# A selective scan whose input products are written where the scan writes, one recurrence ahead, and norms folded into weights

## The chip, the cores and the metric

The program runs on one core of a Trainium2 chip. The core has five engines that work side by side, each with its own queue of instructions: TensorE (PE, matrix products, written to the memory PSUM), VectorE (DVE), ScalarE (ACT), GpSimd (POOL), and SyncE (SP), which here only issues transfers. Operands lie in SBUF, in PSUM or in the chip's main memory (HBM). An instruction waits in its engine's queue until the instructions that it depends on have reported their end; everything behind it in that queue waits too.

The metric is the device time of one execution, in microseconds (us).

## The reference, cut to what matters

The input is four images of 64 channels and 128 x 128 pixels, in float32, and four layers follow one another:

- Layer 0 takes all pixels of all images as one sequence of 65,536 tokens with 64 channels, and applies a selective state-space block (Mamba) with 128 inner channels and 16 states, an output projection, a norm, SiLU, and the residual.
- Layer 1 takes gradients of its input to set a window width, then Fourier-like transforms with small matrix products between them.
- Layer 2 is two 3 x 3 convolutions with batch norm, a channel gate, and the residual.
- Layer 3 is two 3 x 3 convolutions, a Mamba block with 64 states on each image's 16,384 tokens behind a layer norm, and a feed-forward block with a 3 x 3 depthwise convolution behind a second layer norm.

The part that the change touches is the Mamba block and layer 3's norms:

```python
dbl = xc @ x_proj_w.T                   # dt, B and C of each token
delta = softplus(dt @ dt_proj_w.T + dt_proj_b)
def step(h, inp):                       # one token
    d_t, b_t, c_t, u_t = inp
    dA = exp(d_t[..., None] * A)
    h = h * dA + (d_t * u_t)[..., None] * b_t[:, None, :]
    y = einsum('bdn,bn->bd', h, c_t)
    return h, y

def layernorm(x, w, b): return (x - mean) * rsqrt(var + eps) * w + b
t = t + mamba(layernorm(t, ln1_w, ln1_b), ...)
t = t + pvt2ffn(layernorm(t, ln2_w, ln2_b), ...)   # begins with t @ fc1_w.T + fc1_b
```

A Mamba block's input goes through a projection into x and z; x passes a causal convolution of four taps and SiLU and becomes `xc`; the result y is multiplied by SiLU(z).

## The kernel before, in words

**Chunks and iterations.** The class `_Mamba` serves layers 0 and 3. The sequence is cut into chunks of 1024 tokens (TC), 64 in each layer. A recurrence works on one tile of 128 partitions x 1024 tokens: the partitions are 4 states (q) x 32 channels, so that 128 channels are four tiles (j = 0 to 3), and a group of four states (g) is four iterations. Layer 0 has 4 groups, so 16 iterations in a chunk; layer 3 has 16 groups, so 64 iterations.

**An iteration** (in `run`, written out in program order):

1. ScalarE makes `da` = exp(dl x A) (L530), up to four iterations ahead.
2. The input term `bx` = (delta u) x B is made in one of two ways. In an A group ScalarE scales transposed blocks of delta u by B (L373, 32 short passes a group) and TensorE transposes them into PSUM (L470, eight a tile). In a D group TensorE spreads B over the partitions into a PSUM tile `u["B"]` once for the group (L476), and VectorE multiplies it by `du` from SBUF, once an iteration (L561). The product goes to a second PSUM tile, `u["bx"]`, that the group's four iterations use in turn. Layer 0's groups are DADA, layer 3's are DADADAADADADAADA.
3. VectorE runs the scan h = da x h + bx (L567, a `tensor_tensor_scan`), which reads da from SBUF and bx from PSUM, and writes h into one of eight slots of the SBUF tile `ring`.
4. GpSimd multiplies h by C (L570), in the ring's slot and `cb` from SBUF, and writes it back into the slot eight elements lower; once a group it copies the last column of the four slots into `state` (L572).
5. Two and three iterations after a group's end TensorE adds the products over the states into the PSUM tile y (L389), in two halves.

Both PSUM tiles of D groups and those of A groups come from one pool, `bx`, with two buffers. TensorE makes the transposes or the B of iteration i + 1 in iteration i (`produced`).

**Work beside it.** The projections, norms and stores of the chunk before and the chunk ahead are generators (`ahead`, `prepare`, `behind`) that `beside` moves on by pieces between iterations; `yield "wait", k` holds one for k iterations. `pin` fixes each engine's order as written. So nothing is reordered later: what stands behind a late instruction on its engine is late as well.

**Norms of layer 3.** `centred` subtracts the mean with a matrix product, copies the result with ScalarE and squares it; `rstd` makes the reciprocal root; GpSimd multiplies the two (L1273 and L1297); VectorE then applies the norm's scale and term (L1275 into S, the input of the next chunk's projections, and L1299 into o, which the feed-forward reads). S has two columns of the tokens before, zero at an image's begin.

**The gradient stage of layer 1** (L736 to L748) isn't changed; VectorE and GpSimd work there on tiles of some 2048 elements in SBUF.

Of the kernel before, what the change touches and what calls it, by code (L numbers as in the profile page):

```python
# [10 lines left out]
F32 = mybir.dt.float32  # L11
AF = mybir.ActivationFunctionType
ALU = mybir.AluOpType
# [4 lines left out]
P = 128  # L18
B, C, HH, WW = 4, 64, 128, 128
HW = HH * WW  # L20
TC = 1024
# [117 lines left out]
class _Mamba:  # L139
# [19 lines left out]
    def __init__(self, ctx, tc, K, nst, w, kinds, bufs, slots={}):  # L159
        nc = self.nc = tc.nc  # L160
        self.tc = tc
        self.K, self.nst, self.ng, self.kinds, self.bufs = K, nst, nst // NQ, kinds, bufs
        cp = self.cp = ctx.enter_context(tc.tile_pool(name="mc", bufs=1))
        self.wp = ctx.enter_context(tc.tile_pool(name="mw", bufs=2))
        self.dram = ctx.enter_context(tc.tile_pool(name="md", bufs=2, space=DRAM))
        self.bp = ctx.enter_context(tc.tile_pool(name="mb", bufs=1, space=PSUM))
        self.misc = ctx.enter_context(tc.tile_pool(name="mm", bufs=1, space=PSUM))
        self.prev, self.seen = {}, None

        self.slots = slots  # L170

        wx, xpd, dtw = (self.tmp(k)[:n, :DI] for k, n in (("wx", P), ("xpd", 4), ("dtw", 4)))
        for h in range(2):
            nc.sync.dma_start(wx[64 * h : 64 * (h + 1)], w["in_wT"][:, :DI])
        self.taps = []
        for k in range(2):
            cw = cp.tile([P, DI], F32, name=f"cw{k}")
            for h in range(2):
                nc.sync.dma_start(
                    cw[64 * h : 64 * (h + 1)],  # L180
                    w["conv_wT"][2 * k + h : 2 * k + h + 1, :].to_broadcast([64, DI]),
                )
            nc.vector.tensor_mul(cw, wx, cw)
            self.taps.append(cw)
        self.wz = cp.tile([P, DI], F32, name="wz")
        nc.vector.memset(self.wz, 0.0)
        nc.sync.dma_start(self.wz[64:], w["in_wT"][:, DI:])
        self.wbc = cp.tile([P, 2 * nst], F32, name="wbc")
        nc.sync.dma_start(self.wbc, w["xp_bcT"])
        self.wC = cp.tile([P, max(nst, DD)], F32, name="wC")  # L190
        nc.vector.memset(self.wC, 0.0)
        nc.vector.tensor_copy(self.wC[:, :nst], self.wbc[:, nst:])
        self.spread = {}
        for g in (g for g, kind in enumerate(kinds) if kind == "D"):
            s = self.spread[g] = cp.tile([P, P], F32, name=f"spread{g}")
            nc.vector.tensor_copy(
                s.rearrange("p (q e) -> p q e", q=NQ),
                self.wbc[:, NQ * g : NQ * (g + 1)].unsqueeze(2).to_broadcast([P, NQ, DD]),
            )

        nc.sync.dma_start(xpd, w["xp_dt"])
        nc.sync.dma_start(dtw, w["dt_wT"])
        pm = self.pm()
        nc.tensor.matmul(pm[:, :DI], xpd, dtw, start=True, stop=True)
        self.wdt = cp.tile([P, DI], F32, name="wdt")
        nc.vector.tensor_copy(self.wdt, pm[:, :DI])

        cols = {}
        for k in ("conv_b", "dt_b", "D"):
            cols[k] = cp.tile([P, 1], F32, name=f"col_{k}")  # L210
            nc.sync.dma_start(cols[k], w[k])
        self.conv_b, self.dt_b = cols["conv_b"], cols["dt_b"]
        self.dD = cp.tile([P, P], F32, name="dD")
        nc.vector.tensor_scalar(
            self.dD.rearrange("p (j e) -> p j e", j=ND),
            K.eye.rearrange("p (e j) -> p j e", j=ND),
            cols["D"],
            None,
            ALU.mult,
        )  # L220
        self.A = cp.tile([P, ND, self.ng], F32, name="A")
        with nc.allow_non_contiguous_dma(reason="the states on the partitions"):
            for q in range(NQ):
                for j in range(ND):
                    nc.sync.dma_start(
                        self.A[DD * q : DD * (q + 1), j, :],
                        w["A_log"].rearrange("(e j) (g q) -> j q e g", j=ND, q=NQ)[j, q],
                    )
        nc.scalar.activation(self.A, self.A, AF.Exp)
        nc.vector.tensor_scalar_mul(self.A, self.A, -1.0)  # L230
        self.state = cp.tile([P, ND, self.ng], F32, name="state")


        self.ring = cp.tile([P, 2 * ND, GAP + TC], F32, name="ring")

    def pm(self):
        return self.misc.tile([P, TC], F32, name="pm", tag="pm")
# [50 lines left out]
    def inputs(self, c, S, before_silu=None):  # L288

        nc = self.nc  # L290
        xc, sz = c["xc"], c["sz"] = [self.t(k, self.bufs) for k in ("xc", "sz")]
        yield self.slot(c, "z")
        pm = yield from self.halves((self.wz, S[:, 2:]))
        nc.scalar.copy(sz, pm)
        yield self.slot(c, "conv")
        pm = yield from self.halves((self.taps[0], S[:, :TC]), (self.taps[1], S[:, 2:]))

        if before_silu:
            before_silu()
        nc.scalar.activation(xc, pm, AF.Silu, bias=self.conv_b)  # L300
        nc.scalar.activation(sz, sz, AF.Silu)
        nc.scalar.preload_act_table_set(SET6)

    def prepare(self, c):
# [92 lines left out]
    def run(self, chunks, ahead, behind, leads, budget):  # L397
# [109 lines left out]
        for i, (u, j) in enumerate(its):  # L507
# [45 lines left out]
            if full and full[0] <= i:  # L553
                started(behind(full[1], self.gated(full[1])), i)
                full = None
            produced(i + 1)
            if u["kind"] == "D":
                if i == u["at"]:
                    u["bx"] = self.bp.tile([P, TC], F32, name="bx", tag="bx", bufs=2)
                bxs[i] = u["bx"]  # L560
                nc.vector.tensor_mul(bxs[i], u["c"]["du"][j], u["B"])  # L561


            slot = i % (2 * ND)
            hs, hc = self.ring[:, slot, GAP:], self.ring[:, slot, :TC]
            st = self.state[:, j, u["g"] : u["g"] + 1]
            nc.vector.tensor_tensor_scan(  # L567
# [658 lines left out]
def layer3_mamba(ctx, tc, K, w, t3, x3, s3, n3):  # L1226
# [5 lines left out]
    nc.vector.memset(eps, 1e-5)  # L1232
    woT = cp.tile([P, 64], F32, name="woT")
    nc.sync.dma_start(woT, w["out_wT"])
    g1, b1, g2, b2 = (_dup(nc, cp, w[k], f"{k}_") for k in ("ln1_w", "ln1_b", "ln2_w", "ln2_b"))

    def centred(x, out):

        w = x.shape[1]
        pm = yield from m.piece(  # L1240
            *([(lambda pm, a=a: pm[:, a : a + 512], K.cent, x[:, a : a + 512], True, True)] for a in range(0, w, 512))
        )
        nc.scalar.copy(out[0], pm[:, :w])
        nc.scalar.activation(out[1], pm[:, :w], AF.Square)

    tail = cp.tile([P, 2], F32, name="tail")
# [11 lines left out]
    def ahead(c):  # L1258
        if c is chunks[0]:
            load(c)  # L1260
        t0 = c["at"][1]
        S = m.t("S", 1, TC + 2)
        if t0:
            nc.gpsimd.tensor_copy(S[:, :2], tail)
        else:
            nc.gpsimd.memset(S[:, :2], 0.0)
        xs, sq = m.tmp("nxc"), m.tmp("nsq")
        yield from centred(c["X"], (xs, sq))
        if c is not chunks[-1]:
            load(chunks[c["no"] + 1])  # L1270
        yield "wait", 1
        yield from m.rstd(sq, eps)
        nc.gpsimd.tensor_mul(xs, xs, sq)  # L1273
        yield "wait", 2
        nc.vector.tensor_scalar(S[:, 2:], xs, g1, b1, ALU.mult, ALU.add)  # L1275
        if not t0:
            nc.gpsimd.memset(S[:64, 2:3], 0.0)
        nc.gpsimd.tensor_copy(tail, S[:, TC:])
        yield "wait", 1
        yield from m.inputs(c, S)  # L1280

    def behind(c, yg):
        b, t0 = c["at"]
        tr, xr = m.t("tr", 1, 512), m.t("xr", 1, 512)
        for h in range(NH):
            nc.sync.dma_start(tr[64 * h : 64 * (h + 1)], _halves(t3[b], t0)[h])
            nc.sync.dma_start(xr[64 * h : 64 * (h + 1)], _halves(x3[b], t0)[h])
        yield "wait", 2
        pm = yield from m.project(woT, yg, tr)
        nc.scalar.copy(tr, pm[:, :512])  # L1290
        nc.gpsimd.tensor_add(xr, xr, tr)
        yield "wait", 1
        xs, o = m.t("ncr", 1, 512), m.t("o", 1, 512)
        yield from centred(tr, (xs, o))
        yield "wait", 1
        yield from m.rstd(o, eps)
        nc.gpsimd.tensor_mul(o, xs, o)  # L1297
        yield "wait", 2
        nc.vector.tensor_scalar(o, o, g2, b2, ALU.mult, ALU.add)  # L1299
        for h in range(NH):  # L1300
            nc.sync.dma_start(_halves(s3[b], t0)[h], xr[64 * h : 64 * (h + 1)])
            nc.sync.dma_start(_halves(n3[b], t0)[h], o[64 * h : 64 * (h + 1)])
# [6 lines left out]
def layer3_ffn(ctx, tc, K, w, n3, s3, out):  # L1309
# [26 lines left out]
        nc.sync.dma_start(dwb[half[h]], w["dw_b"][:P, :].rearrange("(i q) o -> q (i o)", i=2))  # L1336
    b1 = cp.tile([P, 2], F32, name="ff_fc1_b")
    nc.sync.dma_start(b1, w["fc1_b"].rearrange("(t q) o -> q (t o)", t=2))
    dwb1 = cp.tile([P, 1], F32, name="dwb1")
    nc.sync.dma_start(dwb1, w["dw_b"][P:, :])  # L1340
    nc.sync.dma_start(dww, w["dw_w"].rearrange("(t q) k -> q t k", t=2))
# [212 lines left out]
```

## Time and profile before

| | us |
|---|---|
| median of three runs (20296.65 to 20302.4) | 20297.79 |
| the profiled execution | 20302.69 |
| its span, first to last instruction | 20300.9 |
| VectorE busy | 16466.5 (81%) |
| ScalarE busy | 15261.9 (75%) |
| TensorE busy | 14900.1 (73%) |
| GpSimd busy | 13717.9 (68%) |
| scans, L567 (5120 in the program) | 11153.5 + 610.5 |
| D products, L561 (2304) | 2829.4 |
| GpSimd's products, L570 (5120) | 12134.3 |
| norms' scale and term, L1275 and L1299 (64 each) | 50.7 and 33.4 |

The page shows the span in 40 slices of 507.5 us. Layer 0 fills the first seven, layers 1 and 2 slices 8 to 13, layer 3's Mamba block slices 14 to 37, and the feed-forward block the rest. A digit is an engine's busy share of a slice in tenths. In a row of instructions, the name is line, engine, operation, and tiles (out<-in), with partitions x elements; behind the bar stand busy time, the mean of one in ns, and the engine's idle time just before them with what ended most of it. A timeline's row begins with its start and its length in us.

### The profile page before, as it was taken

The numbers are of one execution on the slowest core, as the hardware profiler recorded it, in microseconds if no ns is written. First come the engines' busy times: TensorE is split into PE (matmuls) and PEld (weight loads), VectorE is DVE, ScalarE is ACT, GpSimd is POOL, SyncE is SP. The second block draws the span as 40 slices with busy tenths as digits, with TensorE's granted clock in tenths as the row PEclk, the third lists the DMA queues.
The fourth block names the chain that finished last, engine by engine and source line by source line (L and its number), as shares of the span: only waits on it lengthen the run. The fifth ranks groups of instructions, "written<-read, shape, count | busy, mean of one in ns | idle before, by whom it ended". The sixth has DMA issues, their size and how long they took to land. (4 is left out here: it accounts for less than half of the span.)

```text
span 20300.9 us, 233291 instructions
## 1 busy us (share of the span) xinstructions
PE 14900.1 (73%) x77130; PEld 7474.5 (37%) x77130; DVE 16466.5 (81%) x9208; ACT 15261.9 (75%) x31389; POOL 13717.9 (68%) x7390
## 2 busy tenths in 40 slices
PE   7777777348798677777777777777777777777677
PEld 3333333147635333333333333333333333333222
DVE  6888888842112799999999999999999999999765
ACT  7888888501122898888898988988989988889522
POOL 6777777710000788888888888888888888888400
PEclk8989998659899888888888888888888888888899
DMA  5555555400121323323323233233232332332211
GB/s 132 143 146 149 145 144 148 96 28 34 39 67 49 80 77 81 86 74 84 82 77 84 77 81 86 74 84 82 77 84 77 82 86 73 84 81 78 57 44 40
DMA packets 687937, 1723.07 MB, mean 85 GB/s; under 512 B 196784, under 2 KB 249344, under 8 KB 681344
## 3 DMA queue, kind: packets, MB, share of 16 engines
q1 hardware_dynamic: 686720, 1708.15, 32.0%
q8 instruction: 605, 9.91, 0.2%
q14 instruction: 612, 5.01, 0.1%
HBM read 1434.79 MB, written 272.63 MB: 84 GB/s over the span
## 5 line engine op out<-in xcount | busy, mean ns | idle before, releaser
L570 POOL TENSOR_TENSOR ring<-ring,cb 128x1024 f32<-128x1024 f32 x5120 | 12134.3, 2388 | 2673.5 <-DVE ring L567 1927.0
L567 DVE TENSOR_TENSOR_SCAN ring<-da,state,bx 128x1024 f32<-128x1024 f32 x4848 | 11153.5, 2336 | 802.6 <-PE bx L470 451.1
L373 ACT ACTIVATE bxT<-duT,BT 128x128 f32<-128x128 f32 x22528 | 7058.0, 387 | 0.0
L530 ACT ACTIVATE da<-dl,A 128x1024 f32<-128x1024 f32 x5120 | 5868.0, 1146 | 1418.2 <-DVE ring L567 1267.6
L470 PE MATMUL bx<-cst,bxT 128*128 128x128 f32 x22528 | 4106.6, 339 | 3093.9 <-DVE bx L561 2526.1
L470 PEld LDWEIGHTS bx<-cst,bxT 128*128 128x128 f32 x22528 | 3473.0, 215 | 4814.7 <-DVE ring L567 1574.0
L389 PE MATMUL y<-ring,cst 128*32 128x512 f32 x20480 | 3560.2, 632 | 311.6 <-POOL ring L570 294.0
L561 DVE TENSOR_TENSOR bx<-du,bx 128x1024 f32<-128x1024 f32 x2304 | 2829.4, 1228 | 225.1 <-DMA du<-d 67.4
L389 PEld LDWEIGHTS y<-ring,cst 128*32 128x32 f32 x20480 | 545.9, 110 | 1863.0 <-POOL ring L570 961.4
L476 PE MATMUL bx<-xc,spread 128*128 128x512 f32 x2304 | 1144.8, 619 | 46.0 <-DVE ring L567 45.0
L1093 PE MATMUL cv<-img,cw 64*64 64x512 f32 x9216 | 1008.0, 594 | 75.2 <-DMA img<-d_x 46.3
L1024 POOL TENSOR_TENSOR xs<-xs,cl 128x1024 f32<-128x1024 f32 x32 | 75.0, 2342 | 1149.6 <-DVE cl L1023 1149.6
L1367 POOL MEMSET h<- 128x18 f32 x64 | 8.3, 132 | 1138.7 <-DVE g L1410 794.2
L1254 POOL MEMSET X<- 64x1 f32 x4 | 0.4, 93 | 1123.0 <-DMA cw<-in_l_conv_wT 1123.0
L1093 PEld LDWEIGHTS cv<-img,cw 64*64 64x64 f32 x9216 | 489.5, 134 | 591.6 <-issue 482.4
L476 PEld LDWEIGHTS bx<-xc,spread 128*128 128x128 f32 x2304 | 390.9, 189 | 830.1 <-DVE ring L567 508.9
L1423 PE MATMUL pd<-h,diag 64*64 64x512 f32 x4608 | 670.5, 629 | 0.7 <-issue 0.7
L567 DVE TENSOR_TENSOR_SCAN ring<-da,bx 128x1024 f32<-128x1024 f32 x272 | 610.5, 2277 | 58.0 <-PE bx L470 42.2
L1007 ACT COPY O<-p 128x1024 f32<-128x1024 f32 x32 | 32.4, 1012 | 803.4 <-PE p L1000 803.4
L1410 DVE SCALAR_TENSOR_TENSOR g<-h,dww,g 128x2048 f32<-128x2048 f32 x256 | 602.0, 2351 | 9.2
L1381 ACT ACTIVATE h<-ph,ff_fc_b 128x384 f32<-128x384 f32 (+1 forms) x384 | 200.1, 574 | 543.9 <-PE ph L1376 543.9
L245 PE MATMUL pm<-xc,wC 128*32 128x512 f32 (+1 forms) x512 | 192.0, 839 | 556.6 <-ACT pos L311 554.2
(309 smaller groups left out, 13655.2 us busy)
## 6 DMA issues: line engine op xcount, KB each, us to landing
cb<-c SPq DMA_DIRECT2D x5120, 128.0 KB, 2.9
dl<-d SPq DMA_DIRECT2D x2048, 128.0 KB, 4.1
du<-d SPq DMA_DIRECT2D x2048, 128.0 KB, 4.4
d<-pos SPq DMA_DIRECT2D x128, 512.0 KB, 2.6
d<-dus SPq DMA_DIRECT2D x128, 512.0 KB, 3.0
X<-d_t SPq DMA_DIRECT2D x124, 256.0 KB, 4.0
S<-in_x SPq DMA_DIRECT2D x120, 256.5 KB, 4.9
res<-in_x SPq DMA_DIRECT2D x128, 128.0 KB, 3.0
```

The costliest lines, as they stand in the source:

```text
L373: nc.scalar.activation(t[:, k, q].rearrange("p e j -> p (e j)"), c["duT"][:, k, :], AF.Copy, scale=c["BT"][:, k, n : n + 1])
L389: nc.tensor.matmul(c["y"][DD * j : DD * (j + 1), _COLS[h]], K.sel, hc[:, _COLS[h]], start=False, stop=u["g"] == self.ng - 1,)
L470: nc.tensor.transpose(bx[:, P * k : P * (k + 1)], v["bxT"][:, k, :, :, j].rearrange("p q e -> p (q e)"), self.K.eye)
L476: nc.tensor.matmul(bx[:, k], self.spread[v["g"]], v["c"]["xc"][:, k], start=True, stop=True)
L530: nc.scalar.activation(das[nexp], v["c"]["dl"][k], AF.Exp, scale=self.A[:, k, v["g"] : v["g"] + 1])
L561: nc.vector.tensor_mul(bxs[i], u["c"]["du"][j], u["B"])
L567: nc.vector.tensor_tensor_scan(hs, das.pop(i), bxs.pop(i), 0.0 if u["c"].get("reset") else st, ALU.mult, ALU.add)
L570: nc.gpsimd.tensor_mul(hc, hs, u["cb"])
L1093: nc.tensor.matmul(p[i][half[h]], W[half[i], k, :], src[half[i], at : at + 4, dx : dx + WW], start=k == 0, stop=k == 8,)
L1381: nc.scalar.activation(himg[:, h * HR + a : h * HR + e, 1 : WW + 1], ph[:, h, a - q : e - q, :], AF.Identity, bias=b1[:, t : t + 1],)
L1410: nc.vector.scalar_tensor_tensor(g1, tap, wk, g1, ALU.mult, ALU.add)
L1423: nc.tensor.matmul(pd[i][half[h]], diag[half[i], k, :], h0[half[i], r : r + 4, dx : dx + WW], start=k == 0, stop=k == 8,)
```

## The change

Three things change.

*D products.* A D group takes no second PSUM tile. The product of an iteration goes into the ring's slot that the scan will write, and the scan reads it from there, in place. The products are issued one recurrence ahead: at j = 0 those of j = 0 and 1, at j = 1 and 2 the next, at j = 3 none.

```diff
             produced(i + 1)
+            slot = i % (2 * ND)
             if u["kind"] == "D":
-                if i == u["at"]:
-                    u["bx"] = self.bp.tile([P, TC], F32, name="bx", tag="bx", bufs=2)
-                bxs[i] = u["bx"]
-                nc.vector.tensor_mul(bxs[i], u["c"]["du"][j], u["B"])
-            slot = i % (2 * ND)
+                for k in range(j + (j > 0), min(j + 2, ND)):
+                    bxs[i - j + k] = self.ring[:, (i - j + k) % (2 * ND), GAP:]
+                    nc.vector.tensor_mul(bxs[i - j + k], u["c"]["du"][k], u["B"])
             hs, hc = self.ring[:, slot, GAP:], self.ring[:, slot, :TC]
```

*The first norm.* Its scale goes into ScalarE's copy of the centred values. Its term is left out of S and added where the projections' results are read: `shift` multiplies the term by the convolution's taps and by z's weights once, and the two SiLU take the result as bias. So that the columns before an image's begin still mean zero, they now hold minus the term.

```diff
+    def shift(self, b):
+        for k, ws in (("conv_b", self.taps), ("z_b", [self.wz])):
+            pm, col = self.pm(), self.cp.tile([P, 1], F32, name=f"{k}_shift")
+            for i, wt in enumerate(ws):
+                self.nc.tensor.matmul(pm[:, :1], wt, b, start=i == 0, stop=i == len(ws) - 1)
+            self.nc.vector.tensor_scalar(col, pm[:, :1], getattr(self, k), None, ALU.add)
+            setattr(self, k, col)
...
-        nc.scalar.activation(sz, sz, AF.Silu)
+        nc.scalar.activation(sz, sz, AF.Silu, bias=self.z_b)
...
-        nc.scalar.copy(out[0], pm[:, :w])
+        nc.scalar.activation(out[0], pm[:, :w], AF.Copy, scale=scale)
...
-            nc.gpsimd.memset(S[:, :2], 0.0)
+            nc.gpsimd.tensor_copy(S[:, :2], pad.to_broadcast([P, 2]))
...
-        nc.gpsimd.tensor_mul(xs, xs, sq)
+        nc.gpsimd.tensor_mul(S[:, 2:], xs, sq)
+        if not t0:
+            nc.gpsimd.tensor_copy(S[:64, 2:3], pad[:64])
+        nc.gpsimd.tensor_copy(tail, S[:, TC:])
         yield "wait", 2
-        nc.vector.tensor_scalar(S[:, 2:], xs, g1, b1, ALU.mult, ALU.add)
-        if not t0:
-            nc.gpsimd.memset(S[:64, 2:3], 0.0)
-        nc.gpsimd.tensor_copy(tail, S[:, TC:])
-        yield "wait", 1
```

*The second norm.* Its scale goes into the feed-forward's first weights and its term, through those weights, into their bias, once before the first strip; `behind` stores GpSimd's product.

```diff
-        yield "wait", 2
-        nc.vector.tensor_scalar(o, o, g2, b2, ALU.mult, ALU.add)
+        yield "wait", 3
...
+    g, n = (_dup(nc, cp, w[k], f"ff_{k}") for k in ("ln2_w", "ln2_b"))
+    ph = hp.tile([P, 2, 4, WW], F32, name="ph", tag="ph")
+    for t in range(2):
+        nc.tensor.matmul(ph[:, t, 0, :1], f1[half[0], t, :], n[half[0]], start=True, stop=True)
+    nc.vector.tensor_add(b1, b1, ph[:, :, 0, 0])
+    nc.vector.tensor_scalar(f1, f1, g, None, ALU.mult)
```

More of the change, by code (lines that the diff above doesn't have):

```diff
@@ L211, in __init__ @@
             nc.sync.dma_start(cols[k], w[k])
-        self.conv_b, self.dt_b = cols["conv_b"], cols["dt_b"]
+        self.conv_b, self.dt_b, self.z_b = cols["conv_b"], cols["dt_b"], 0.0
         self.dD = cp.tile([P, P], F32, name="dD")
@@ L1234, in layer3_mamba, with centred @@
     nc.sync.dma_start(woT, w["out_wT"])
-    g1, b1, g2, b2 = (_dup(nc, cp, w[k], f"{k}_") for k in ("ln1_w", "ln1_b", "ln2_w", "ln2_b"))
-    def centred(x, out):
+    g1, b1 = (_dup(nc, cp, w[k], f"{k}_") for k in ("ln1_w", "ln1_b"))
+    m.shift(b1)
+    pad = cp.tile([P, 1], F32, name="pad")
+    nc.vector.tensor_scalar_mul(pad, b1, -1.0)
+    def centred(x, out, scale=1.0):
         w = x.shape[1]
@@ L1265, in ahead @@
         else:
-            nc.gpsimd.memset(S[:, :2], 0.0)
+            nc.gpsimd.tensor_copy(S[:, :2], pad.to_broadcast([P, 2]))
         xs, sq = m.tmp("nxc"), m.tmp("nsq")
-        yield from centred(c["X"], (xs, sq))
+        yield from centred(c["X"], (xs, sq), g1)
         if c is not chunks[-1]:
```

## The prediction, on record before the changed kernel ran

> **What bounds the kernel now.** I read the slices first. VectorE is at nines in slices 15 to 37, which is layer 3's recurrence; layer 0's (slices 1 to 7) has it at eights.
>
> ```profile
> DVE  6888888842112799999999999999999999999765
> POOL 6777777710000788888888888888888888888400
> ```
>
> Then the same as a table over inner stretches of both stages (PE, PEld, DVE, ACT, POOL busy):
>
> ```profile
> 978.00:3709.00 2731.00, 2153.95 (x10062) 996.75 (x10058) 2283.78 (x1222) 2397.91 (x4607) 2138.09 (x1129) 0.90 0.57 146
> 6900.00:18680.00 11780.00, 8509.86 (x40434) 4218.77 (x40432) 11189.35 (x5848) 10572.87 (x22787) 9925.19 (x5305) 0.85 0.31 81
> ```
>
> In layer 3 VectorE is busy 95%, ScalarE 90%, GpSimd 84%. The scans recorded from 7000 to 18500 us (3614 + 192) are 59.5 chunks of 64, so a chunk takes 11500 / 59.5 = 193.3 us; GpSimd works 0.8425 x 193.3 = 162.9 us of it. Layer 0's stretch holds 376 products, 8 in a chunk: 47 chunks, 58.1 us each, with 45.5 us of GpSimd.
>
> Third, the groups: the scan, the D product before it, GpSimd's product behind it.
>
> ```profile
> L570 POOL TENSOR_TENSOR ring<-ring,cb 128x1024 f32<-128x1024 f32 x5120 | 12134.3, 2388 | 2673.5 <-DVE ring L567 1927.0
> L567 DVE TENSOR_TENSOR_SCAN ring<-da,state,bx 128x1024 f32<-128x1024 f32 x4848 | 11153.5, 2336 | 802.6 <-PE bx L470 451.1
> L561 DVE TENSOR_TENSOR bx<-du,bx 128x1024 f32<-128x1024 f32 x2304 | 2829.4, 1228 | 225.1 <-DMA du<-d 67.4
> ```
>
> Fourth, VectorE's timeline in layer 3: two D recurrences and a run of eight A scans (start, us).
>
> ```profile
> 10023.89 1.23 DVE L561 TENSOR_TENSOR bx<-du,bx 128x1024 f32<-128x1024 f32 x1
> 10025.22 2.35 DVE L567 TENSOR_TENSOR_SCAN ring<-da,state,bx 128x1024 f32<-128x1024 f32 x1
> 10027.60 1.23 DVE L561 TENSOR_TENSOR bx<-du,bx 128x1024 f32<-128x1024 f32 x1
> 10028.93 18.01 DVE L567 TENSOR_TENSOR_SCAN ring<-da,state,bx 128x1024 f32<-128x1024 f32 x8
> ```
>
> A D recurrence costs 10027.60 - 10023.89 = 3.71 us: the scan starts 1.33 after its product and the next product 2.38 after the scan, each waiting for the other's result. Scans with no such wait follow at (18.01 - 2.35) / 7 = 2.24 us. GpSimd's own timeline beside that A run:
>
> ```profile
> 10033.90 9.41 POOL L570 TENSOR_TENSOR ring<-ring,cb 128x1024 f32<-128x1024 f32 x4
> 10043.23 0.22 POOL L572 COPY state<-ring 128x4 f32<-128x4 f32 x1
> 10043.38 9.38 POOL L570 TENSOR_TENSOR ring<-ring,cb 128x1024 f32<-128x1024 f32 x4
> ```
>
> Its pitch is 2.34 us: in A groups it falls behind the scans and catches up only in D groups, where 3.71 leaves it idle 1.36 each time.
>
> The view that decides is the timeline of layer 1's gradient stage, the one place where VectorE has operations with two SBUF inputs while GpSimd works.
>
> ```profile
> 3837.81 4.63 POOL L736 TENSOR_TENSOR v<-X 128x2112 f32<-128x2112 f32 x1 [7.49 <-DMA X<-d_x]
> ...
> 3849.17 2.28 DVE L743 TENSOR_TENSOR gy<-d 128x2048 f32<-128x2048 f32 x1
> ...
> 3891.25 6.74 POOL L739 TENSOR_TENSOR d<-X 128x2112 f32<-128x2112 f32 x1
> 3893.43 6.71 DVE L743 TENSOR_TENSOR gy<-d 128x2048 f32<-128x2048 f32 x1
> 3897.95 6.54 POOL L747 TENSOR_TENSOR gx<-gx,gy 128x2048 f32<-128x2048 f32 x1
> 3900.06 6.58 DVE L741 TENSOR_TENSOR gx<-v 128x2048 f32<-128x2048 f32 x1
> ```
>
> Alone, L743 takes 2.28 us and a GpSimd operation of this size 4.63. Together each takes 6.5 to 6.7, one starting 2.2 after the other, in strict turns: the pair's period is 3900.06 - 3893.43 = 6.63, the sum of both. They exclude each other; what VectorE adds is 6.63 - 4.59 (the pitch of GpSimd's L736 to L739 alone, 3837.81 to 3842.40) = 2.04 us for 2048 elements.
>
> **What the Trainium skill says.** "SBUF — State Buffer", section "Who interferes with whom": a DVE instruction with two SBUF inputs contends with a GpSimd instruction that reads SBUF, since its second input comes through the read interface that both share; section "SBUF: two separate sides" calls it an exclusive lock for the whole instruction. The gradient stage agrees (6.63 above). The first section also says that a DVE instruction with at most one SBUF input, outside the 2-port modes, does not contend: the trace agrees, since scans (da in SBUF, bx in PSUM) and GpSimd's products run side by side at 2.35 and 2.37 us. It names no scan; none with two long SBUF inputs runs beside GpSimd here, so its case is inferred.
>
> **The change part by part.**
>
> *The order.* Product, product, scan, product, scan, product, scan, scan. No scan follows its own product at once, and no product waits for a scan that reads its destination. The product then costs what yg (L593: PSUM and SBUF in, SBUF out) does between starts, 1.14 us (980.46 to 981.60), the scan 2.24: 3.38 for 3.71, a gain of 0.33 x 2304 = 760 us of VectorE if nothing else held it. The product still reads one operand from PSUM, so it doesn't contend. Product j+1 now stands ahead of scan j, and so does its wait for du; du's waits are 67 us in all, and its loads are issued several iterations ahead: 0, at worst these 67 again. Its ring slot was last used eight iterations back; 0 while GpSimd is under three behind.
>
> *The place.* The D scan's second input moves from PSUM to the ring, SBUF. It now has two SBUF inputs, and each of GpSimd's products reads two. By the gradient stage they exclude each other: 2304 scans, each holding the port for about 2.1 us (2.04 for 2048 elements; the scan's pitch of 2.24 us for 1024 says two cycles for each, so as long). The unknown is this hold: 0 if scans don't take the port, 2.35 if it lasts to the scan's end. I take 2.1.
>
> What is late next is GpSimd, which everything waits for: products feed PE's sums (L389), and behind the sums in PE's order stand the next group's transposes or B. So its work and the holds cannot overlap, and its backlog from A groups has nowhere to go. Layer 3, a chunk: 162.9 + 28 x 2.1 = 221.7, plus some 2.5 in which GpSimd waits for neither's turn (first products of D groups, which start 2.52 after their scan, as 9998.79 to 10001.31 now, though the port is free at 2.1: 0.4 x 7) = 224.2, against 193.3: +30.9 x 64 = +1978 us. Layer 0: 45.5 + 8 x 2.1 = 62.3, plus 3 that stay of GpSimd's present longest gap (5.8 to 6.8 us where yg waits for PE, less a hold and what PE gains while D runs slower), 65.3 against 58.1: +7.2 x 64 = +461 us. The 760 of VectorE are not lost but hidden: VectorE no longer sets the pace.
>
> *PSUM's bx.* D groups need one buffer where they took two, so the next A group's transposes can run before the D group ends. L567's waits for PE (451 us) shrink; behind GpSimd this is worth 0, without the contention at most some 250.
>
> *The norms.* L1275 (64 x 0.71 us between starts) and L1299 (64 x 0.44) go: 74 us of VectorE, 0 on the path if GpSimd sets it. The scale in ScalarE's copy: the same pass, 1.01 us. GpSimd's product count stays; its few small copies change by under 10 us in all. S is ready about an iteration earlier: 0.
>
> *Setup.* Matmuls of one column, [P,1] additions, a scaling of 256 elements; the four ln2 loads move from before layer 3 into the feed-forward's start, ahead of dww on SP's queue: 4 x 0.6 issue, +3 us.
>
> Sum: 1978 + 461 + 3 = +2442 on the profiled execution's 20302.7 (span 20300.9): 22745; the median stands 5 below it: 22740.
>
> **The rivals.**
>
> *No contention (0.10): faster.* The scan might take its inputs otherwise than a tensor_tensor. Then layer 3's chunk loses 28 x 0.33 = 9.2, 1.15 of norms and some of 2.9 waits for PE (177.7 / 61): to about 182, above ScalarE's 173.5: -11.3 x 64 = -723. Layer 0, whose waits for PE stay, some -2 x 64 = -130. 19450. It decides if the hold is under about 1.0 us: (193.3 - 162.9 - 2.5) / 28 = 1.0 in layer 3, and layer 0 has 58.1 - 45.5 - 3 = 9.6 / 8 = 1.2, so below this GpSimd stays under the old pace.
>
> *Port shared element by element (0.05): about the same.* The scan needs an element every second cycle; GpSimd might take the others and lose half: 28 x 1.05 = 29.4, so 192 a chunk beside 193.3. 20300, within 250.
>
> *GpSimd's backlog is absorbed (0.13): slower, by less.* Only the D recurrence's own length counts: 2.1 + 2.34 = 4.44 for 3.71, +0.73 x 2304 = 1680, less some 100 of waits and norms: 21880. Against it: GpSimd has no slack in A groups (2.34 for 2.24) and 162.9 of 193.3 in all.
>
> **How the numbers follow.** The full ledger has 0.72; its own range is 22250 to 23350 (a hold of 2.04 to 2.35 gives -138 to +576; the gaps of 2.5 and 3 us, from none to double, 352 either way). With the absorbed case the range is 21700 to 23400. Chances: slower 0.72 + 0.13 + 0.01 = 0.86, within 0.2% (about what a measurement of this kernel tells from no change) 0.03, faster 0.11.
>
> **What would show it.** Right: the groups split into scans with "bx" at 2.34 us and 2304 scans with "ring" as second input well above it, 3.5 us or more in the mean, waiting included; GpSimd's L570 mean rising from 2.39 to about 3.2 and GpSimd busy over 95% in layer 3, with D recurrences 4.4 us apart; layer 3's chunk near 224, layer 0's near 65. Products near 1.2 us show the order's gain was real. Wrong: ring scans at 2.35 and GpSimd's products at 2.39; then 19450. A chunk near 218 with idle GpSimd means absorption.

## The result and the profile after

The changed kernel takes 22418.3 us (median of four, 22415.2 to 22419.3) where the kernel before takes 20297.5: 1.1044 of it, 95% interval 1.1025 to 1.1063. That is slower by 2121 us, 322 less than forecast and inside the range. The profiled execution's span is 22416.7 us.

The slices of the changed kernel: VectorE is at nines as before, and GpSimd is at eights in layer 3 and up to nines in layer 0.

```profile
DVE  7889888822116999999999999999999999999866
POOL 7998889700005888888888888888888888888600
```

Two inner stretches (PE, PEld, DVE, ACT, POOL busy), layer 0 and layer 3:

```profile
978.00:3709.00 2731.00, 2121.66 (x9379) 1012.00 (x9382) 2433.82 (x1135) 2233.23 (x4276) 2459.75 (x1049) 0.86 0.53 136
7500.00:20000.00 12500.00, 8391.31 (x37338) 3963.37 (x37337) 11778.88 (x5288) 9799.54 (x21038) 10970.88 (x4900) 0.81 0.27 70
```

In layer 3 GpSimd's share rises from 84 to 88%, and ScalarE's falls from 90 to 78%: it waits for the others now. VectorE's stays near 95%, but what fills it is shown by the groups, by form:

```profile
L576 DVE TENSOR_TENSOR_SCAN ring<-da,state,ring 128x1024 f32<-128x1024 f32 x2184 | 7463.2, 3432 | 0.0
L576 DVE TENSOR_TENSOR_SCAN ring<-da,state,bx 128x1024 f32<-128x1024 f32 x2664 | 6078.0, 2327 | 948.1 <-PE bx L479 898.2 <-ACT da L539 31.6 <-ACT bxT L382 11.1
L571 DVE TENSOR_TENSOR ring<-du,bx 128x1024 f32<-128x1024 f32 x2304 | 2723.7, 1203 | 283.5 <-PE bx L485 183.9 <-DMA du<-d 92.1 <-issue 3.3
```

The scans of A groups, with bx in PSUM, take 2.33 us as ever. Those of D groups, with their input in the ring, are recorded at 3.43. The product is 0.025 us shorter. GpSimd's groups:

```profile
L579 POOL TENSOR_TENSOR ring<-ring,cb 128x1024 f32<-128x1024 f32 x5120 | 13148.2, 2591 | 2203.3 <-DVE ring L576 1837.0 <-PE bx L479 204.5 <-DMA cb<-c 66.6
L581 POOL COPY state<-ring 128x4 f32<-128x4 f32 x1280 | 1354.0, 1058 | 0.0
```

In the mean its products are up from 2.39 to 2.59 us, and the copy of four elements from 0.20 to 1.06. Where this comes from, one D group shows; first VectorE's timeline, then GpSimd's over the same time.

```profile
12037.48 2.33 DVE L571 TENSOR_TENSOR ring<-du,bx 128x1024 f32<-128x1024 f32 x2
12039.73 3.83 DVE L576 TENSOR_TENSOR_SCAN ring<-da,state,ring 128x1024 f32<-128x1024 f32 x1
12043.48 1.19 DVE L571 TENSOR_TENSOR ring<-du,bx 128x1024 f32<-128x1024 f32 x1
12044.60 3.68 DVE L576 TENSOR_TENSOR_SCAN ring<-da,state,ring 128x1024 f32<-128x1024 f32 x1
12048.20 1.19 DVE L571 TENSOR_TENSOR ring<-du,bx 128x1024 f32<-128x1024 f32 x1
12049.31 5.88 DVE L576 TENSOR_TENSOR_SCAN ring<-da,state,ring 128x1024 f32<-128x1024 f32 x2
```

```profile
12041.34 2.20 POOL L581 COPY state<-ring 128x4 f32<-128x4 f32 x1
12043.78 2.35 POOL L579 TENSOR_TENSOR ring<-ring,cb 128x1024 f32<-128x1024 f32 x1 [0.24 <-PE bx L479]
12048.45 2.35 POOL L579 TENSOR_TENSOR ring<-ring,cb 128x1024 f32<-128x1024 f32 x1 [2.32 <-DVE ring L576]
```

GpSimd's products of the A group end at 12041.3. Only then does the first scan run, to 12043.56, and GpSimd's tiny copy behind it is recorded at 2.20 us. The product from 12043.78 to 12046.13 comes next; the second scan, recorded from 12044.60, ends at 12048.28, so it runs 2.15 us after the product's end. The engines take turns, 4.71 us from scan to scan (12044.60 to 12049.31), where a D recurrence cost 3.71. The fourth scan follows the third at once: no product stands between them, so VectorE is back before GpSimd has seen the third scan's end, and GpSimd's two products from 12053.12 on take 6.56 us.

It is the same all through layer 3. GpSimd's means mix two cases, as the rows over the whole run show (behind the count, min/median/max in ns):

```profile
L581 POOL COPY state<-ring x1280: 180/202/2309, 92.8 to 21174.3; 128x4 f32<-128x4 f32 x183
L579 POOL TENSOR_TENSOR ring<-ring,cb x5120: 2334/2375/4442, 79.6 to 21172.0; 128x1024 f32<-128x1024 f32 x197
```

The medians are nearly those of before (195 and 2372). But 550 copies took over 2 us and 567 products over 3: they met a scan. Where GpSimd meets it between two of its operations, it pauses. From 7500 to 20000 us it pauses 624 times for more than 0.6 us, and in each of these pauses a D scan ends, 2.11 to 2.16 us after GpSimd's last operation.

By layer, from the first scan's start to the last one's (layer 0 has 1024 scans, layer 3 has 4096; last column the whole span):

| us | layer 0 | a chunk | layer 3 | a chunk | span |
|---|---|---|---|---|---|
| before | 3727.5 | 58.2 | 12368.7 | 193.3 | 20300.9 |
| changed | 4003.9 | 62.6 | 14210.3 | 222.0 | 22416.7 |

### The profile page after: what moved, and what is told of

The parts are those of the page before. It is cut to its first block, busy times and chain, and to the rows that moved or that the text cites. A ratio compares the mean times of both kernels' runs of the same rounds, so it can differ in the third digit from the quotient of the medians.

```text
span 22416.7 us, 233249 instructions
## 1 busy us (share of the span) xinstructions
PE 15674.7 (70%) x77140; PEld 7666.3 (34%) x77140; DVE 18564.3 (83%) x9085; ACT 15312.0 (68%) x31389; POOL 16443.8 (73%) x7390
## 5 line engine op out<-in xcount | busy, mean ns | idle before, releaser
L579 POOL TENSOR_TENSOR ring<-ring,cb 128x1024 f32<-128x1024 f32 x5120 | 13148.2, 2591 | 2203.3 <-DVE ring L576 1837.0
L576 DVE TENSOR_TENSOR_SCAN ring<-da,state,ring 128x1024 f32<-128x1024 f32 x2184 | 7463.2, 3432 | 0.0
L576 DVE TENSOR_TENSOR_SCAN ring<-da,state,bx 128x1024 f32<-128x1024 f32 x2664 | 6078.0, 2327 | 948.1 <-PE bx L479 898.2
L479 PE MATMUL bx<-cst,bxT 128*128 128x128 f32 x22528 | 4211.5, 339 | 3547.9 <-DVE ring L576 2070.1
L398 PE MATMUL y<-ring,cst 128*32 128x512 f32 x20480 | 4162.2, 672 | 681.8 <-POOL ring L579 678.3
L571 DVE TENSOR_TENSOR ring<-du,bx 128x1024 f32<-128x1024 f32 x2304 | 2723.7, 1203 | 283.5 <-PE bx L485 183.9
L398 PEld LDWEIGHTS y<-ring,cst 128*32 128x32 f32 x20480 | 651.8, 114 | 2618.2 <-POOL ring L579 1636.7
L581 POOL COPY state<-ring 128x4 f32<-128x4 f32 x1280 | 1354.0, 1058 | 0.0
```

What stands on the lines that cost most here:

```text
L398: nc.tensor.matmul(c["y"][DD * j : DD * (j + 1), _COLS[h]], K.sel, hc[:, _COLS[h]], start=False, stop=u["g"] == self.ng - 1,)
L479: nc.tensor.transpose(bx[:, P * k : P * (k + 1)], v["bxT"][:, k, :, :, j].rearrange("p q e -> p (q e)"), self.K.eye)
L571: nc.vector.tensor_mul(bxs[i - j + k], u["c"]["du"][k], u["B"])
L576: nc.vector.tensor_tensor_scan(hs, das.pop(i), bxs.pop(i), 0.0 if u["c"].get("reset") else st, ALU.mult, ALU.add)
L579: nc.gpsimd.tensor_mul(hc, hs, u["cb"])
L581: nc.gpsimd.tensor_copy(self.state[:, :, u["g"]], self.ring[:, slot - j : slot + 1, GAP + TC - 1])
```

## The experiments

Two questions were open. The first is whether the port is the cause. The *port theory* says that a D scan with two SBUF inputs and a GpSimd operation that reads SBUF exclude each other; its rivals are that a scan from the ring, or in place, is slow by itself, or that running ahead moved a wait. The second is what the order and the norms' edits are worth where the port is out of the way. Every time below stands beside 20299 to 20310 for the kernel before on the same chip.

### The parts apart

The norms' edits alone, on the kernel before. Its D products are kept; the lines show what differs from the changed kernel:

```diff
-                for k in range(j + (j > 0), min(j + 2, ND)):
-                    bxs[i - j + k] = self.ring[:, (i - j + k) % (2 * ND), GAP:]
-                    nc.vector.tensor_mul(bxs[i - j + k], u["c"]["du"][k], u["B"])
+                if i == u["at"]:
+                    u["bx"] = self.bp.tile([P, TC], F32, name="bx", tag="bx", bufs=2)
+                bxs[i] = u["bx"]
+                nc.vector.tensor_mul(bxs[i], u["c"]["du"][j], u["B"])
```

> The norms' edits alone, D products as before. If VectorE sets layer 3's pace before the change, its 64 x 0.71 and 64 x 0.44 us leave the path: 74 us, 20224. If they were covered, 20297. A value above 20300 would mean that the edits cost something elsewhere (three iterations of waiting, transfers at the feed-forward's start).

Measured 20311.0 us, ratio 1.0008 (1.0000 to 1.0016): nothing came off. VectorE's work did fall, but its waits took its place. The same stretch of layer 3, before and with the norms' edits (third column VectorE):

```profile
7500.00:18000.00 10500.00, 7588.90 (x36056) 3762.86 (x36053) 9973.01 (x5214) 9426.60 (x20315) 8848.80 (x4732) 0.85 0.31 81
```

```profile
7500.00:18000.00 10500.00, 7588.68 (x36050) 3786.80 (x36048) 9909.71 (x5102) 9432.14 (x20306) 8813.95 (x4730) 0.85 0.30 81
```

TensorE's, ScalarE's and GpSimd's columns are the same to 0.7% or better, VectorE's is 63 us lower: the chunks pass at the old rate, so VectorE's work alone wasn't the pace.

The D products' edit alone, norms as before:

```diff
-                if i == u["at"]:
-                    u["bx"] = self.bp.tile([P, TC], F32, name="bx", tag="bx", bufs=2)
-                bxs[i] = u["bx"]
-                nc.vector.tensor_mul(bxs[i], u["c"]["du"][j], u["B"])
+                for k in range(j + (j > 0), min(j + 2, ND)):
+                    bxs[i - j + k] = self.ring[:, (i - j + k) % (2 * ND), GAP:]
+                    nc.vector.tensor_mul(bxs[i - j + k], u["c"]["du"][k], u["B"])
```

> The D products' edit alone, norms as before. Port theory (D scans and GpSimd's reads exclude each other, and GpSimd's work plus the holds fill the chunk): VectorE's 74 us of norms come back but are mostly hidden, 22420 to 22490. If the norms' edits did part of the slowing, clearly below 22400.

Measured 22481.3 us, ratio 1.1077 (1.1060 to 1.1094): the whole loss is in this part, and the norms' edits, worth nothing alone, are worth 63 us here (22481.3 - 22418.3; layer 3's stretch is 14290.8 us with the norms' operations and 14210.3 without). The second norm's operation gives a likely reason, in the groups of this kernel:

```profile
L1299 DVE TENSOR_SCALAR o<-o,ln_w__37345,ln_b__37348 128x512 f32<-128x512 f32 x64 | 158.8, 2482 | 9.7 <-POOL o L1297 9.7
```

It took 0.52 us before; here it waits for GpSimd too: 63 of the 64 end 0.28 us after the end of a GpSimd product. It has one SBUF tensor; the Trainium skill, "SBUF — State Buffer", section "Who interferes with whom", lists `tensor_scalar` among the operations that can take the shared port in a 2-port mode, and 2.48 us beside 0.52 agrees. How this becomes 63 us isn't shown: what GpSimd loses beside the two norms' operations (its products there are recorded at 2.85 and 2.52 us for 2.38) is some 40.

The place without the order, on the changed kernel:

```diff
-                for k in range(j + (j > 0), min(j + 2, ND)):
-                    bxs[i - j + k] = self.ring[:, (i - j + k) % (2 * ND), GAP:]
-                    nc.vector.tensor_mul(bxs[i - j + k], u["c"]["du"][k], u["B"])
+                bxs[i] = self.ring[:, slot, GAP:]
+                nc.vector.tensor_mul(bxs[i], u["c"]["du"][j], u["B"])
```

> The changed kernel, but each D product is issued just ahead of its own scan, still into the ring. Port theory: the place decides, so no faster than 22418. The pause between two scans of a D group then always lets GpSimd in, also ahead of the fourth, which follows the third at once in the changed kernel: 1.33 + 3 x 4.7 + 2.25 = 17.7 for a group's 16.8, 576 groups: up to +520, 22400 to 22950. If running ahead is what costs (a wait that moved), below 21500.

Measured 22371.8 us, ratio 1.1023 (1.1008 to 1.1038), 28 below the lowest value that was expected and 47 below the changed kernel: the added turns cost nothing. The place alone makes the loss; running ahead under contention is worth nothing (layer 3 28 us better with it, layer 0 47 us worse, where single executions with the same layer 0 differ by up to 25 us: 4003.9 in the changed kernel, 3979.0 in the run before this one). That the fourth scan slips in at once saves no time; a likely reason is that GpSimd has that work still to do.

### The port taken away

GpSimd's product is replaced by a filling of the same place, which reads nothing; in the changed kernel and, as a control, in the kernel before.

```diff
-            nc.gpsimd.tensor_mul(hc, hs, u["cb"])
+            nc.gpsimd.memset(hc, 0.0)
```

> The changed kernel, but GpSimd fills its half of the ring's slot with zeros where it multiplied by C (the product by C is left out): it writes the same place at the same point of the order and reads nothing. Port theory: D scans no longer wait, 2.3 us each for 3.4, D recurrences 3.38 us apart, 19300 to 19700. If a scan is slow because its input lies in SBUF or because it works in place, it stays slow: 22000 or more.

> The kernel before with the same filling in place of the product by C (left out here too): the control. GpSimd isn't what sets the pace before the change, so 20100 to 20300. Port theory: the changed kernel's counterpart is faster than this one by 500 to 850 us, the sign of the change turned round; otherwise slower by about 2100.

Measured 20128.7 us (0.9913, 0.9899 to 0.9928) and 20195.2 us (0.9947, 0.9932 to 0.9962). The changed kernel becomes 2290 us faster. That is not the contention's price alone, since a filling takes GpSimd 0.96 us where a product takes 2.34; the control's 108 us say what the lighter work is worth only where GpSimd doesn't set the pace. What tells is the scans' own time. The D scans of layer 3, min/median/max in ns, in the changed kernel and then without GpSimd's reads:

```profile
L576 DVE TENSOR_TENSOR_SCAN ring<-da,state,ring x1240: 2317/3642/4529, 7496.4 to 17983.4; 128x1024 f32<-128x1024 f32 x178
```

```profile
L576 DVE TENSOR_TENSOR_SCAN ring<-da,state,ring x1456: 2318/2343/4324, 7516.9 to 17992.8; 128x1024 f32<-128x1024 f32 x182
```

So a scan from the ring and in place is as fast as one from PSUM, 2.34 us, as long as GpSimd doesn't read. The few at 4.3, 169 of 2304 in both layers, all stand beside GpSimd operations that still do (L347 and L355 most of all), and these work on other tiles: it isn't the shared ring that makes the two engines meet. A GpSimd operation that only writes doesn't get in the way: 502 of the D scans ran beside a whole filling, in 2.32 us. A filling as long as the product wasn't tried. D recurrences are 3.38 us apart there (12018.58 to 12021.95 to 12025.33), as worked out. The sign turns, as the port theory says: 66 us faster than the control. The size does not: 500 to 850 were expected. Some contention is left: the 169 scans cost VectorE some 270 us, 164 of them in layer 3. VectorE also waits longer: in layer 3 its work, these 164 included, is 206 us shorter than the control's (11740 to 11534), its pauses are 144 longer (526 to 670). In the whole run it waits 889.5 us before A scans, 767.2 of them for TensorE's transposes.

TensorE's granted clock also fell with the change, from 0.85 to 0.81 in layer 3's stretches. It isn't the cause: without GpSimd's reads it is 0.83, lower than before too, and that run is the fastest.

### GpSimd's slack

Two more passes a chunk in layer 3, 300 us in all, on a tile that nothing reads any more:

```diff
         nc.gpsimd.tensor_add(xr, xr, tr)
+        for _ in range(2):
+            nc.gpsimd.tensor_mul(yg, yg, yg)
```

> The changed kernel with two more passes of GpSimd over 128 x 1024 elements a chunk in layer 3, on a tile that nothing reads any more: 64 x 2 x 2.34 = 300 us of GpSimd work. If its work and the holds fill each chunk, all of it shows: +300, 22720. If VectorE's own alternation with it sets the pace and GpSimd has slack, +0 to 100.

> The kernel before with the same two passes: the control. GpSimd has 30 us of 193 to spare in a chunk, so 0 to +60.

Measured 22615.0 us for the changed kernel, 197 more, and 20326.5 us for the kernel before, 24 more (ratio 1.0011, 1.0005 to 1.0018). In layer 3's stretch it is +216 and +9. GpSimd sets most of the pace after the change and none before; about a quarter of added work still finds room.

### D groups without a second SBUF input

On the norms' edits: B is spread anew for every iteration, and the product replaces it in its PSUM tile.

```diff
-            if v["kind"] == "A" or i == v["at"]:
-                bx = bxs[i] = self.bp.tile([P, TC], F32, name="bx", tag="bx", bufs=2)
+            bx = bxs[i] = self.bp.tile([P, TC], F32, name="bx", tag="bx", bufs=2)
...
-            elif i == v["at"]:
-                v["B"] = bx
+            else:
                 for k in _COLS:
...
-                nc.vector.tensor_mul(bxs[i], u["c"]["du"][j], u["B"])
+                nc.vector.tensor_mul(bxs[i], u["c"]["du"][j], bxs[i])
```

> The norms' edits with another form of D group: TensorE spreads B anew for each iteration, and the product replaces B in its own PSUM tile, so that a product no longer waits for the scan before it, and no scan has a second SBUF input. A D recurrence then costs 1.33 + 2.26 = 3.59 for 3.71: 0.12 x 2304 = 276 us, and 74 of norms: 19950 if TensorE's extra 1728 x 1.24 us stay hidden; 20200 or more if the new B comes late (it can start only when the scan two before has ended).

Measured 20349.2 us, ratio 1.0026 (1.0016 to 1.0035): no gain, as expected if B comes late. Layer 3's stretch falls by 74 us against before (12294.5), layer 0's rises by 114 (3841.4): there products wait 225 us for B, before 8, and the product by SiLU(z) (yg) waits 287, before 232.

### What sets the pace before

These were meant to lighten ScalarE in layer 3 by leaving out SiLU and with it two table loads a chunk; in the kernel before, with the norms' edits, and in the changed kernel without GpSimd's reads (the product by C left out there as well).

```diff
-        nc.scalar.activation(xc, pm, AF.Silu, bias=self.conv_b)
-        nc.scalar.activation(sz, sz, AF.Silu)
-        nc.scalar.preload_act_table_set(SET6)
+        f = AF.Silu if self.slots else AF.Identity
+        nc.scalar.activation(xc, pm, f, bias=self.conv_b)
+        nc.scalar.activation(sz, sz, f)
+        if self.slots:
+            nc.scalar.preload_act_table_set(SET6)
```

> The kernel before with a lighter burst of ScalarE in layer 3: the two SiLU of a chunk become plain copies with bias (SiLU is left out), so that both table loads of 1.28 us go: 64 x 2.56 = 164 us of ScalarE. VectorE's own work is unchanged. If VectorE's work alone set the pace, 0. If ScalarE's bursts hold A groups back, up to -164: 20140.

> The same lightening (SiLU left out in layer 3) with the norms' edits. They brought nothing in front of the full burst. If ScalarE's burst swallowed their 74 us, this run is up to 74 below the one without the norms' edits; if something else paces both, equal.

> The changed kernel with GpSimd's filling in place of the product by C and the lightened burst of ScalarE in layer 3 (product by C and SiLU left out). If ScalarE is what took the order's gain of up to 760 us once the contention was gone, more than its own 164 us come off 20129: 19800 to 19960. If TensorE or the pieces' order took it, 0 to -164.

Measured 20667.7 us (1.0176, 1.0160 to 1.0191), 20532.7 us (1.0107, 1.0090 to 1.0124) and 20367.2 us (1.0028, 1.0019 to 1.0038): all slower. The profile tells that the edit did the reverse of what it was for. Without the preload of a table set that holds both functions, a logarithm and an exponential that follow one another in layer 3 each load their own; the table loads of the lightened kernel before:

```profile
L132 ACT ACT_TABLE_LOAD x132 | 169.4, 1283 | 50.1 <-DMA c_b__31453<-in_l_c_b 41.0 <-issue 3.9 <-DMA bn_v__31471<-in_l_bn_v 2.9
L133 ACT ACT_TABLE_LOAD x132 | 169.4, 1283 | 2.3
L532 ACT ACT_TABLE_LOAD x65 | 83.4, 1283 | 4.8 <-DMA dl<-d 3.7
L315 ACT ACT_TABLE_LOAD x64 | 82.1, 1283 | 1.2
```

The kernel before has five loads each on L132 and L133. In all there are 254 more loads, 326 us of ScalarE. Read that way it is an answer: layer 3's stretch of the kernel before grew from 12368.7 to 12716.5, by 348 us. ScalarE, 90% busy, had no room, although VectorE was the busier. The same addition costs 229 us in the changed kernel without reads (12204.3 to 12433.6). That the norms' edits bring 117 us in layer 3 beside the heavier ScalarE (12599.1) and nothing beside the usual one isn't explained.

The last run takes work from ScalarE and gives it to VectorE, on the norms' edits:

```diff
-        nc.scalar.copy(sz, pm)
+        nc.vector.tensor_copy(sz, pm)
```

> The norms' edits, D products as before, and the copy of z's projection out of PSUM (one of 128 x 1024 a chunk, 1.0 us) moved from ScalarE to VectorE in both Mamba layers. If ScalarE's passes set the pace, as the additional table loads suggest, 64 to 128 us come off 20311: 20180 to 20250, below the kernel before. If VectorE's work does, its 128 x 1.2 us come on top: 20390 to 20460. About 20311 if neither does alone.

Measured 20429.4 us, ratio 1.0061 (1.0047 to 1.0075), as if VectorE set the pace; by layer it is two answers. Layer 3 falls by 81 us against the norms' edits alone (12381.2 to 12300.5), for 63 us less of ScalarE and 77 more of VectorE. Layer 0 rises by 191 (3737.8 to 3928.9): there the copy stands on VectorE ahead of the scans and waits for TensorE, in the groups of this run:

```profile
L303 DVE COPY sz<-pm 128x1024 f32<-128x1024 f32 x128 | 155.1, 1211 | 212.8 <-PE pm L254 212.8
```

No run beats the kernel before with the whole computation in it. The copy on VectorE in layer 3 alone would be some 70 us faster than before by these stretches; it wasn't tried.

## Why the prediction was right, and where it was not

**The contention** was the step that decided, and it holds. It was inferred for the scan from the gradient stage, where no scan runs. Taking GpSimd's reads away brings the ring's scans back from 3.64 to 2.34 us in the median.

**The hold** of 2.1 us is right: 2.15 from the end of GpSimd's operation to the scan's in the timeline above and in the median of layer 3's 624 pauses. It was carried over from an addition of 2048 elements to a scan of 1024, which takes about twice as long for an element (2.24 us from start to start, a product of 1024 takes 1.12), and that held. So falls the rival of a port shared element by element, which had put the hold at 1.05.

**The ledger** (GpSimd's work plus the holds) gave 221.7 us a chunk in layer 3 and 62.3 in layer 0; measured are 222.0 and 62.6. Mis-sized are the gaps put on top, 2.5 and 3 us: the balance leaves 0.3 for each. (5.5 - 0.6) x 64 = 314 us is the forecast's excess, nearly all of 322. The gaps are gone because GpSimd, always behind, has next to none: all its pauses over 0.6 us from 7500 to 20000 are holds, and so are 249 of its 270 us of pauses from 978 to 3709, in layer 0. That the sum closes so well is in part luck: with the norms' operations still there, a chunk of layer 3 takes 223.3. The ledger is a good sum, but not a strict bound: a quarter of the added passes found room, and the 2.32 us that GpSimd waits in D groups are the hold with some 0.2 of signals.

**The signs by which to know it** were half wrong. The scans' 3.43 us came close to "3.5 or more". GpSimd over 95% busy and its products at 3.2 us did not come: 88% and 2.59. Only part of the holds stretches a product; another part shows as pauses, waits for the scan's result (1837 us in the whole run), and another sits in short operations: 1100 us in the 1280 state copies, as much as in the 5120 products (1014). Turns within a group are 4.71 us, not 4.4, and one of the four has none.

Two figures don't follow from their own terms. A chunk under absorption would be 193.3 + 28 x 0.73 = 213.7 us, not 218. And the ledger's range ends at 23350, where the hold and the gaps together would give 22740 + 576 + 352 = 23668, while its lower end counts both. Neither matters at 222.0 us and 22418.

**What bounds the kernel before** is the step that failed. VectorE's 95% was taken for the pace, so that 760 us of order and 74 of norms would come through if nothing held them. Neither does. The norms' edits alone bring nothing; the whole change with most of the contention gone brings, against the control, 62 us in layer 3 (12266.2 to 12204.3) and 5 in layer 0. More work for ScalarE shows in full, and less of it shortens layer 3 though VectorE gets more. A likely account is that the three are coupled: TensorE's transposes need ScalarE's scaled blocks, and VectorE's longest waits in layer 3 are for these two (159 and 83 us from 7500 to 18000); ScalarE in turn makes da only when a scan has freed a buffer. No run takes the three apart. The error didn't reach the forecast, since all this lies behind GpSimd after the change; the rival without contention was mis-sized by it: 19450, where the nearest run, with GpSimd's reads gone, has 20129 (some 270 us of VectorE's time in it are contention that is left).

**The norms under contention** were put at nothing behind GpSimd; they are worth 63 us, probably because their operations wait for GpSimd too.

**The absorbed rival**, 21880, fell: GpSimd's added work shows after the change by 216 us of 300 in layer 3, before it by 9. That GpSimd has no slack in A groups was the right argument.

## What to carry to other kernels

Before a VectorE operand moves from PSUM to SBUF, count the SBUF inputs that remain: with two, the scans here and the additions of the gradient stage took turns with GpSimd's operations that read SBUF, and the cost was the sum of GpSimd's time and the holds, not the longer of the two engines' times. An engine that is 95% busy need not set the pace; where buffers couple three engines, try a small cut on each before working for a large one. And a table set that is preloaded saves loads far from where it stands: look at the count of loads after touching it.

## What the runs showed of the hardware

- A `tensor_tensor_scan` with two SBUF inputs keeps GpSimd operations that read SBUF out for 2.15 us of the 2.34 that it takes for 1024 elements, though it needs about twice as long for an element as a product (2.24 us from start to start beside 1.12); a filling GpSimd operation (0.96 us) doesn't hinder it.
- A GpSimd copy of four elements that meets such a scan is recorded at 2.2 us instead of 0.2 (550 of 1280 in the changed kernel).
- A VectorE `tensor_scalar` of 128 x 512 elements with one SBUF tensor, 0.52 us before, took 2.48 us in the mean where it came upon GpSimd's products in the run of the D products' edit alone; 63 of 64 ended 0.28 us after a product did.
